# Splitting a norm and some maskings between engines, and a new order of loads, in a planned transformer kernel

## Chip, cores and metric

The kernel runs on one core of a Trainium2 chip. The metric is the device time of one execution in microseconds (us); of several executions the median is taken. The engines are called by their short names as well: PE is TensorE, DVE is VectorE, ACT is ScalarE, POOL is GpSimd and SP is SyncE, which here only issues DMAs.

## What is computed

Two sequences of 1024 tokens with 128 features pass six blocks, all in float32. Cut to what matters:

```python
x = x + 0.5 * L0_ffn(layernorm(x))            # mixes each token with the one before
x = x + L0_attn(layernorm(x))                 # 8 heads, full softmax
x = x + 0.5 * L0_ffn(layernorm(x))
x = x + 0.5 * L1_ffn(x)                       # "moe a": 16 experts, the best 2 for each token
x = x + L1_attn(x)                            # "scan": linear attention with decay
x = x + 0.5 * L1_ffn(x)                       # "moe b": the same experts once more
```

The scan keeps a state of 16 x 16 for each head, `state = state * beta + alpha * (k outer v)`, and its output is `q @ state`. An expert is `gelu(layernorm(h @ W1 + b1) * g1 + be1) @ W2 + b2`, weighted with the normalised router probability.

## The kernel before

The tokens lie in four groups G of 512 (four tiles of 128 tokens), two for each of the two sequences ("batches" b). All stages are generators that yield where they have to wait. A planner (`Plan`, from L74) keeps a modelled time of each engine and of each tile, and `step` takes the stage whose next piece can begin first. Engines run their instructions in the order in which the planner wrote them, so its constants decide the order on each engine: `SOON` (L82) is how far ahead it looks for a more urgent stage once attention is over, `late` and `delay` (L179 to L189) push a stage back, `note` (L134 to L169) is the modelled cost of an instruction, 0.45 us for a DMA issued by SP. LATE and GATHER at the end of the kernel give each stage of moe a, scan and moe b its delay; `behind` delays a quad by its turn.

Where TensorE would wait in the model, `Warm._fill` (L246 to L260) issues matmuls on zeros ("fillers", line L260 in the profile).

The stages that the change and the prediction touch:

- `norm` takes statistics on DVE, adds eps, and GpSimd raises to the power -0.5 (`rs`). Each of four tiles is then scaled by the engine named in `by`. A tile on ScalarE needs a bias, `sh = -mean * rs`, which GpSimd makes in two instructions. The norm of the scan's input has `by = ["DVE", "ACT"] * 2`; that of moe b, in `logits("b", ...)` at the end of `scan_out`, has `["DVE"] * TG`, all four on DVE.
- `route` finds for each token its two experts and its two rows in a table of slots in DRAM (`pos`), all on DVE with a few matmuls (`pc`). `scatter` (line L926 in the profile) writes the normed tokens to these rows (`x_slots`), 8 indirect DMAs for a group, issued by GpSimd one after the other. The pool queue is in order: a scatter, a power or a masking stands behind all that was written to GpSimd before it.
- `choose` finds which expert each of the extra 15 tiles belongs to (`eid`), and `quad` handles four tiles of 128 slots. For the first four quads the expert matrices lie in SBUF; the others fetch theirs with one DMA a tile (`wt<-w`), for which SP reads `eid`. Then SP loads the slots (`xg<-x_slots`), TensorE transposes (`pxT`), multiplies (`ph`), DVE and GpSimd make the norm (`hst`, `hmv`, `hrs`), DVE or ScalarE scales (`hn`, the split is chosen by the model), TensorE transposes (`phT`), ScalarE applies gelu (`act`), TensorE multiplies (`py`), and SP stores `y_slots<-y`.
- `gather` brings each token's two outputs back (`yt<-y_slots`), 16 indirect DMAs for a batch, issued by GpSimd; `combine` adds them to x on DVE, and in moe b SP stores the result.
- `scan_in` norms and transposes; `scan_pair` makes q and k of two chunks of 128 tokens, rotates them (`tm` on DVE, `qk` on GpSimd), scales and transposes them, and makes the scores in four banks `pj`. Each bank, 128 x 512, is masked with the causal matrix on DVE (`aj`), 16 maskings a batch. `scan_state` makes the states `S` from `pkv`, `scan_out` the outputs `po`, `oT_scan`, `pw`, and `x_scan` on DVE.

The order in the last 290 us is: moe a for batch 0 and 1, the scan of batch 0 while moe a of batch 1 ends, the scan of batch 1, moe b of batch 0 and 1, and the last gathers.

Each fetched matrix and the slot loads of a quad are issued so:

```python
for i, e in enumerate(experts_of(sp, eid, q)):
    ins = sp.dma_start(out=wt[:, i, :], in_=w12[bass.ds(e, 1), :, :].rearrange("a c d -> c (a d)"))
    ...
yield wait(("sent", s, 2 * b), ("sent", s, 2 * b + 1), banks=0, on="SP", issued=not own)
```

Of the kernel before, what the change touches and what calls it, by code (L numbers as in the profile page):

```python
# [14 lines left out]
ALU = mybir.AluOpType  # L15
# [7 lines left out]
TG = 4  # L23
# [9 lines left out]
def bc(ap, axis, n):  # L33

    u = ap.unsqueeze(axis)
    shape = list(u.shape)
    shape[axis] = n
    return u.to_broadcast(shape)
# [35 lines left out]
class Plan:  # L74
# [4 lines left out]

    by_engine, SOON = False, 0.3  # L82

    slow = 1.1
    RATE = 250.0
# [48 lines left out]
    def note(self, engine, op, args, kwargs):  # L134

        aps = [*args, *kwargs.values()]
        aps = [v.ap if isinstance(v, bass.IndirectOffsetOnAxis) else v for v in aps]
        aps = [v for v in aps if hasattr(v, "tensor")]
        out = kwargs.get("out", aps[0])

        ins = [v for v in aps if v is not out and v.space != DRAM]
        begin = self.free.get(engine, 0.0)
        for v in ins:
            hop = 0.0 if self.by.get(self._name(v)) == engine else self.HOP
            begin = max(begin, self.wrote.get(self._name(v), 0.0) + hop)
        if out.space == PSUM:
            begin = max(begin, self.wrote.get(self._name(out), 0.0))
        if "dma" in op:
            issued = max(begin, self.begun) + (1.25 if engine == "POOL" else 0.45)
            size = min(math.prod(out.shape), math.prod(kwargs["in_"].shape))  # L150
            moved = 4e-3 * size / self.RATE
            self.free["DMA"] = max(issued + 0.4, self.free.get("DMA", 0.0)) + moved
            end = self.free["DMA"] + 2.0
        else:
            issued = end = begin + (
                1.04 if ALU.pow in args else self.length(engine, op, out, ins)
            )
        self.free[engine] = issued
        for v in ins:
            k = self._name(v)  # L160
            self.used[k] = max(self.used.get(k, 0.0), end)
        k = self._name(out)
        self.wrote[k], self.by[k] = end, None if "dma" in op else engine
        self.used[k] = max(self.used.get(k, 0.0), end)
        self.end = max(self.end, end)
        self.issued = max(self.issued, issued)
# [49 lines left out]
def wait(*flags, **more):  # L216
    return {"for": flags, **more}
# [20 lines left out]
class Warm(Timed):  # L238
# [4 lines left out]
    zeros, ident, on = None, None, False  # L243
# [30 lines left out]
def kernel(ctx: ExitStack, tc: tile.TileContext, a, out):  # L274
# [5 lines left out]
    plan = Plan()  # L280
    in_order = InOrder(tc, nc.gpsimd)
    pe = Warm(plan, "PE", nc.tensor)
    dve, act, pool, sp = (
        Timed(plan, name, engine)
        for name, engine in (
            ("DVE", nc.vector), ("ACT", nc.scalar), ("POOL", in_order),
            ("SP", nc.sync),
        )
    )
# [32 lines left out]
    def tiles_of(t):  # L322
        return t.rearrange("p (n d) -> p n d", d=D)
# [139 lines left out]
    causal = const.tile([P, P], F32, name="causal", tag="causal")  # L463
# [81 lines left out]
    def norm(G, x, xn, by, twice=False):  # L545

        st = stat.tile([P, TG, nc.vector.BN_STATS_DIM], F32, tag=f"st{G}", name="st4")
        mv = stat.tile([P, TG, 2], F32, tag=f"mv{G}", name="mv4")
        for n in range(TG):
            latest["stats"] = dve.bn_stats(st[:, n, :], x[:, n, :]).ins  # L550
            dve.bn_aggr(mv[:, n, :], st[:, n, :])
        rs = stat.tile([P, TG], F32, tag=f"rs{G}", name="rs4")
        e = pool if "DVE" not in by else dve
        if twice:


            e.tensor_scalar(rs, mv[:, :, 1], 1.0 + EPS, EPS * EPS, ALU.mult, ALU.add)
        else:
            e.tensor_scalar(rs, mv[:, :, 1], EPS, None, ALU.add)
        if ("tile pools",) in plan.flags:  # L560
            yield wait(banks=0, on="POOL")
        pool.tensor_tensor(rs, rs, half_neg, ALU.pow)
        if "ACT" in by:
            sh = stat.tile([P, TG], F32, tag=f"sh{G}", name="sh4")
            pool.tensor_tensor(sh, mv[:, :, 0], rs, ALU.mult)
            pool.tensor_scalar(sh, sh, -1.0, None, ALU.mult)
        yield wait(banks=0, on=by[0])
        for n in range(TG):
            scale = rs[:, n : n + 1]
            if by[n] == "ACT":  # L570
                act.activation(
                    xn[:, n, :], x[:, n, :], AF.Identity, bias=sh[:, n : n + 1], scale=scale
                )
            else:
                engines[by[n]].tensor_scalar(
                    xn[:, n, :], x[:, n, :], mv[:, n, 0:1], scale, ALU.subtract, ALU.mult
                )
        yield wait(on="PE")
# [163 lines left out]
    xb_of, xm_of, xs_of, xn_of, xT_b, z_of, route_of = {}, {}, {}, {}, {}, {}, {}  # L742
# [273 lines left out]
    WINDOW, AHEAD = 6, 8  # L1016
# [9 lines left out]
    def quad(s, b, q, turn):  # L1026
# [3 lines left out]
        if own:  # L1030
            yield wait(
                ("w12",), ("tile pools",),
                *([("quad", turn - AHEAD)] if turn >= AHEAD else []), banks=0, on="SP",
            )
            mats = [(res["w1"][:, 4 * q + i, :], res["w2"][:, 4 * q + i, :]) for i in range(n)]
        else:
            yield wait(
                ("eid", s, b), ("tile pools",),
                *([("quad", turn - AHEAD)] if turn >= AHEAD else []), banks=0, on="SP",
            )  # L1040
            eid = eid_of[s, b]
            wt = tp.tile([P, TG, 2 * D], F32, tag=f"w{q % 4}", name="wt")
            for i, e in enumerate(experts_of(sp, eid, q)):
                ins = sp.dma_start(
                    out=wt[:, i, :], in_=w12[bass.ds(e, 1), :, :].rearrange("a c d -> c (a d)")
                )
                after(ins.ins, moved)
                if i < n - 1:
                    yield wait(on="SP", banks=0, issued=True, late=1.0)
            mats = [(wt[:, i, 0:D], wt[:, i, D:]) for i in range(n)]  # L1050
# [241 lines left out]
    def scan_pair(b, pair):  # L1292
# [49 lines left out]
        pj = [bank("pj") for j in range(4)]  # L1342
# [11 lines left out]
        for j in range(4):  # L1354
            where, tag = AM[pair % 2][j]
            aj = where.tile([P, 2, 2, P], F32, tag=tag, name="aj")
            dve.tensor_tensor(
                aj.rearrange("p i m t -> p (i m) t"), tiles_of(pj[j]), bc(causal, 1, 4), ALU.mult
            )
            done(pj[j])  # L1360
            am.append(aj)
        st["am", pair] = am
# [34 lines left out]
    def scan_out(G):  # L1397
# [37 lines left out]
        done(pw)  # L1435
        plan.set("scanned", G)
        yield wait(banks=0, on="DVE")
        yield from logits("b", G, xs_of[G], ["DVE"] * TG, "ACT")

# [243 lines left out]

    def behind(turn, late):

        return lambda: late + 0.8 * max(0, turn - sum(f[0] == "quad" for f in plan.flags))


    LATE = {"a": (2.0, 0.0), "scan": (-1, 0.5), "b": (3, 0.5)}
    GATHER = {"a": (0, 1), "b": (1.0, 1)}
    for s in ("a", "b"):
        for b in range(NB):
            late_by = LATE[s][b]
# [119 lines left out]
```

## Time and profile before

| | |
|---|---|
| median of 3 runs | 632.66 us (631.8 to 632.89) |
| the profiled execution | 633.37 us, of which its span is 631.3 |
| PE busy | 567.6 us (90%), 4418 matmuls |
| DVE busy | 461.9 us (73%), 1448 instructions |
| ACT busy | 291.3 us (46%), 626 |
| POOL busy | 284.9 us (45%), 345 |
| maskings `aj<-pj,causal` | 32 on DVE, 679 to 686 ns, between 446.1 and 516.2 us |
| norm of moe b `xn_moe_b` | 16 on DVE, 336 to 503 ns |
| biases `sh` of the scan's norm | on POOL, 198 to 202 ns and 228 to 238 ns (median) |
| fetched matrices `wt<-w` | 60 of 128 KB, 2.2 us to landing |
| slot loads `xg<-x_slots` | 32 (28 of 256 KB), 4.3 us to landing |
| indirect DMAs of POOL | 64 scatters and 64 gathers, near 1 us of issue each |

The span runs from the first to the last instruction. A group's busy time is the sum of its instructions; neighbours on one engine overlap in part, so the step from one to the next can be shorter than one lasts. The granted clock is that of TensorE, as a share of full speed.

### The profile page before, as it was taken

Reading aid. Unit: us, or ns where it says so; the run is one execution under the profiler, and the core shown is the slowest. Engines: PE = TensorE matmul, PEld = TensorE weight load, DVE = VectorE, ACT = ScalarE, POOL = GpSimd, SP = SyncE. Lnnn points to the kernel's source line nnn. Section 1 sums busy time; section 2 is a strip of 40 time slices with the busy share of each in tenths; the row PEclk is TensorE's granted clock in tenths of the full one; section 3 lists DMA queues with packets and bytes.
Section 4 is the critical chain, followed back from the end, with each engine's and each line's share of the span. In section 5 each row is a group of like instructions: output and inputs, shape, how many; then the busy total and the mean of one; then the engine's idle time right before and its main releaser. Section 6 shows DMA issues by size and latency. Waiting matters only on the chain.

```text
span 631.3 us, 12216 instructions
## 1 busy us (share of the span) xinstructions
PE 567.6 (90%) x4418; PEld 344.8 (55%) x4418; DVE 461.9 (73%) x1448; ACT 291.3 (46%) x626; POOL 284.9 (45%) x345
## 2 busy tenths in 40 slices
PE   8899999999999999989998998888897999999930
PEld 6664433333333434333346886777666867978820
DVE  6748887777867787788317883887897896777742
ACT  2442456655655465544781663575121201377720
POOL 5653000002613356204633847855744532675875
PEclk9887999999999999999998999999999896799985
DMA  4087000000202001000006437621200107237742
GB/s 121 4 295 202 1 2 2 1 1 1 69 2 67 1 1 35 1 2 9 26 2 179 123 102 205 177 73 42 65 9 1 35 23 219 86 101 227 225 120 72
DMA packets 62894, 46.22 MB, mean 73 GB/s; under 512 B 6241, under 2 KB 57841, under 8 KB 62833
## 3 DMA queue, kind: packets, MB, share of 16 engines
q1 hardware_dynamic: 58210, 36.78, 20.0%
q0 software_dynamic: 4096, 8.40, 4.7%
q8 instruction: 35, 0.57, 0.4%
q10 hardware_dynamic: 528, 0.26, 0.2%
q14 instruction: 25, 0.20, 0.1%
HBM read 26.94 MB, written 19.53 MB: 74 GB/s over the span
## 4 chain that ended last, share of the span: by engine, by line
PE 60%; DVE 21%; POOL 9%; issue 6%; DMA 3%; ACT 2%; POOLq 0%; ACTq 0%; DVEq 0%
PE sT L265 17%; PE av L265 10%; PE sc L265 7%; POOL x_slots L926 2%; POOL yt L65 2%; DVE tmp L233 2%; PE ph L265 2%; DVE hst L233 2%; PE py L265 2%; PE pk L265 2%; PE pt L260 2%; DMA yt<-y_slots,pos_moe_b 2%; PE pr L265 2%; PE pt L270 2%; DVE aj L233 2%
## 5 line engine op out<-in xcount | busy, mean ns | idle before, releaser
L233 DVE TENSOR_REDUCE tmp<-sc 128x1 f32<-128x512 f32 x256 | 162.3, 684 | 48.3 <-PE sc L265 47.9
L233 ACT ACTIVATE pT<-sT 128x512 f32<-128x512 f32 x256 | 137.7, 596 | 106.8 <-PE sc L265 85.6
L265 PE MATMUL sc<-kT,qT 32*128 32x512 f32 x512 | 151.8, 642 | 1.6 <-DVE rv L233 1.1
L265 PE MATMUL sT<-q,kT 32*128 32x512 f32 x512 | 135.4, 639 | 0.7 <-issue 0.7
L265 PE MATMUL av<-pT,va 128*32 128x256 f32 x1024 | 80.8, 390 | 0.0
L265 PEld LDWEIGHTS av<-pT,va 128*32 128x32 f32 x1024 | 21.2, 108 | 90.4 <-issue 89.1
L265 PEld LDWEIGHTS sT<-q,kT 32*128 32x128 f32 x512 | 37.7, 183 | 43.4 <-issue 29.8
L65 POOL TENSOR_TENSOR x_attn<-att,x_ffn_a 128x512 f32<-128x512 f32 x4 | 5.1, 1272 | 119.3 <-DVE att L233 119.3
L265 PEld LDWEIGHTS sc<-kT,qT 32*128 32x128 f32 x512 | 47.3, 185 | 15.4 <-ACT pT L233 6.1
L233 ACT ACTIVATE act<-phT,be,g 128x128 f32<-128x128 f32 x124 | 46.0, 465 | 8.7 <-PE phT L270 7.6
L926 POOL DMA_INDIRECT x_slots<-xn_moe_b,pos_moe_b x32 | 31.7, 991 | 29.2 <-issue 26.7
L926 POOL DMA_INDIRECT x_slots<-xn_moe_a,pos_moe_a x32 | 32.7, 1020 | 22.6 <-issue 14.2
L65 POOL TENSOR_TENSOR hrs<-hrs,half_neg 128x4 f32<-128x4 f32 (+1 forms) x32 | 32.7, 1022 | 11.0 <-DVE hrs L233 10.2
L65 POOL TENSOR_TENSOR rs<-rs,half_neg 128x4 f32<-128x4 f32 x24 | 25.3, 1054 | 23.7 <-DVE rs L233 22.6
L65 POOL DMA_INDIRECT yt<-y_slots,pos_moe_a x32 | 31.7, 991 | 9.4 <-issue 5.3
L65 POOL DMA_INDIRECT yt<-y_slots,pos_moe_b x32 | 31.1, 971 | 10.0 <-issue 6.2
L233 DVE BATCH_NORM_STATS2 hst<-ph 128x6 f32<-128x128 f32 x124 | 27.5, 283 | 5.2 <-PE ph L265 5.2
L270 PE MATMUL phT<-ident,hn 128*128 128x128 f32 x124 | 25.4, 296 | 5.6 <-DVE hn L233 4.2
L233 ACT COPY xgT<-pxT 128x512 f32<-128x512 f32 (+1 forms) x29 | 16.5, 581 | 27.9 <-PE pxT L270 27.9
L233 ACT ACTIVATE hn<-ph,hrs 128x128 f32<-128x128 f32 x55 | 17.1, 368 | 22.7 <-DVE hn L233 15.0
L233 DVE TENSOR_SCALAR hn<-ph,hrs 128x128 f32<-128x128 f32 x69 | 20.2, 343 | 7.7 <-POOL hrs L65 7.5
L233 DVE SCALAR_TENSOR_TENSOR x_moe_b<-yt,gate_moe_b,x_moe_b 128x128 f32<-128x128 f32 x32 | 11.1, 353 | 16.9 <-DMA yt<-y_slots,pos_moe_b 16.6
(362 smaller groups left out, 1082.9 us busy)
## 6 DMA issues: line engine op xcount, KB each, us to landing
wt<-w SPq DMA_DIRECT2D x60, 128.0 KB, 2.2
xg<-x_slots SPq DMA_DIRECT2D x28, 256.0 KB, 4.3
y_slots<-y SPq DMA_DIRECT2D x28, 256.0 KB, 2.6
x_slots<-zeros SPq DMA_DIRECT2D x2, 1792.0 KB
w_last<-in_w SPq DMA_DIRECT2D x1, 1024.0 KB, 16.9
w<-in_w SPq DMA_DIRECT2D x1, 1024.0 KB
w<-w SPq DMA_DIRECT2D x1, 1024.0 KB
out<-x_moe_b SPq DMA_DIRECT2D x4, 256.0 KB
```

Source lines behind the costliest of these rows:

```text
L65: r = method(*args, **kwargs)
L233: return method(*args, **kwargs)
L260: self._engine.matmul(*args, **kw)
L265: return self._engine.matmul(out, lhsT, rhs, **kwargs)
L270: return self._engine.transpose(out, in_, ident)
L926: ins = in_order.unordered.indirect_dma_start(**kw)
```

## The change

Four things are edited. A masking may go to ScalarE (a copy from PSUM to SBUF) and GpSimd (the multiplication, in place), where the model has these two finish it no later than DVE. The norm of moe b is done half by ScalarE, and once attention is over the bias is one DVE instruction in place of two on GpSimd. A fetched matrix is modelled as a longer issue and its stage gets `late=6.0`, so that slot loads can come in front of it on SP. And the planner's constants are set anew.

```diff
-    by_engine, SOON = False, 0.3
+    by_engine, SOON = False, 0.5
...
-            issued = max(begin, self.begun) + (1.25 if engine == "POOL" else 0.45)
+            moving = out.tensor.name.startswith("wt")
+            issued = max(begin, self.begun) + (
+                1.25 if engine == "POOL" else 0.65 if moving else 0.5
+            )
...
         if "ACT" in by:
             sh = stat.tile([P, TG], F32, tag=f"sh{G}", name="sh4")
-            pool.tensor_tensor(sh, mv[:, :, 0], rs, ALU.mult)
-            pool.tensor_scalar(sh, sh, -1.0, None, ALU.mult)
+            if ("tile pools",) in plan.flags:
+                yield wait(banks=0, on="DVE")
+                dve.scalar_tensor_tensor(sh, mv[:, :, 0], -1.0, rs, ALU.mult, ALU.mult)
+            else:
+                pool.tensor_tensor(sh, mv[:, :, 0], rs, ALU.mult)
+                pool.tensor_scalar(sh, sh, -1.0, None, ALU.mult)
...
-                *([("quad", turn - AHEAD)] if turn >= AHEAD else []), banks=0, on="SP",
+                *([("quad", turn - AHEAD)] if turn >= AHEAD else []), banks=0, on="SP", late=6.0,
...
-            dve.tensor_tensor(
-                aj.rearrange("p i m t -> p (i m) t"), tiles_of(pj[j]), bc(causal, 1, 4), ALU.mult
-            )
+            flat = aj.rearrange("p i m t -> p (i m) t")
+
+            if plan.free["DVE"] + 0.68 < max(plan.free["ACT"] + 0.84, plan.free["POOL"]) + 1.22:
+                dve.tensor_tensor(flat, tiles_of(pj[j]), bc(causal, 1, 4), ALU.mult)
+            else:
+                act.copy(flat, tiles_of(pj[j]))
+                pool.tensor_tensor(flat, flat, bc(causal, 1, 4), ALU.mult)
...
-        yield from logits("b", G, xs_of[G], ["DVE"] * TG, "ACT")
+        yield from logits("b", G, xs_of[G], ["DVE", "ACT"] * 2, "ACT")
...
-        return lambda: late + 0.8 * max(0, turn - sum(f[0] == "quad" for f in plan.flags))
+        return lambda: late + 0.6 * max(0, turn - sum(f[0] == "quad" for f in plan.flags))
...
-    LATE = {"a": (2.0, 0.0), "scan": (-1, 0.5), "b": (3, 0.5)}
-    GATHER = {"a": (0, 1), "b": (1.0, 1)}
+    LATE = {"a": (2.0, 0.0), "scan": (-1.0, 0.5), "b": (2.0, 0.5)}
+    GATHER = {"a": (0.0, -2.0), "b": (1.0, 1.0)}
```

Counted over all instructions as the two kernels are built: of 32 maskings 10 go to ScalarE and GpSimd (4 of batch 0, 6 of batch 1); 8 of the 16 tiles of moe b's norm go to ScalarE; 8 biases are made by DVE, and GpSimd makes 4 fewer pairs. By the planner's choice 13 of 55 `hn` go from ScalarE to DVE, and 85 fillers are issued instead of 89. The order of the instructions differs throughout the last 290 us.

## The prediction

> **What bounds the kernel now.** I read the page, then busy time in stretches of 5 us, then the chain of waits and the timelines of those stretches. On the page no single engine is the bound.
>
> ```profile
> span 631.3 us, 12216 instructions
> ...
> PE 60%; DVE 21%; POOL 9%; issue 6%; DMA 3%; ACT 2%; POOLq 0%; ACTq 0%; DVEq 0%
> ...
> L65 POOL TENSOR_TENSOR x_attn<-att,x_ffn_a 128x512 f32<-128x512 f32 x4 | 5.1, 1272 | 119.3 <-DVE att L233 119.3
> ```
>
> Up to about 340 us (attention) the two kernels issue the same instructions in the same order but for a few swaps, so the change acts on the last 290 us. The stretches show what limits there. Columns: length; PE, weight load, DVE, ACT and POOL busy with counts; granted clock; DMA share; GB/s.
>
> ```profile
> 440.00:445.00 5.00, 5.00 (x65) 4.61 (x63) 1.78 (x7) 3.53 (x11) 3.78 (x5) 1.00 0.28 78
> 445.00:450.00 5.00, 4.81 (x86) 3.86 (x78) 4.86 (x13) 0.00 (x0) 3.78 (x5) 1.00 0.25 65
> 460.00:465.00 5.00, 4.74 (x66) 2.65 (x57) 4.93 (x13) 0.67 (x2) 0.51 (x1) 1.00 0.07 16
> 505.00:510.00 5.00, 3.91 (x53) 2.20 (x43) 4.77 (x14) 0.00 (x0) 0.00 (x0) 1.00 0.00 0
> 525.00:530.00 5.00, 5.00 (x20) 4.08 (x19) 3.53 (x19) 0.93 (x4) 1.15 (x2) 0.50 0.70 197
> 540.00:545.00 5.00, 5.00 (x27) 5.00 (x25) 2.59 (x17) 1.76 (x3) 3.78 (x5) 0.52 0.17 56
> 545.00:550.00 5.00, 5.00 (x42) 4.87 (x41) 3.39 (x17) 2.10 (x6) 3.22 (x4) 1.00 0.13 41
> ```
>
> VectorE is full in both scans (445 to 465, 495 to 520) while ScalarE is empty and GpSimd has holes. From 525 to 545 TensorE is full at half clock. The chain shows the hole on GpSimd in the second scan, and the end:
>
> ```profile
> 503.94 9.19 issue
> 513.12 0.96 POOL x_slots L926
> ...
> 625.11 2.49 DMA yt<-y_slots,pos_moe_b
> 627.68 0.35 DVE x_moe_b L233
> ```
>
> The end is GpSimd's: 16 gathers of the last batch, 1.26 us apart, start when the last batch's expert outputs are stored (604.98). Whatever brings that point forward moves the end by as much.
>
> **The masked scores.** Of 32 maskings 10 leave VectorE: 4 of 16 in the first scan, 6 in the second. One takes 681 ns, four in a row 2.48 us, so each is worth (2.48 - 0.68)/3 = 0.60. For the first scan that is 2.4 us, for the second 3.6. What they cost elsewhere: a ScalarE copy of 128x512 from PSUM (0.58, the row of oT_scan), on an engine that idles there, and 1.27 on GpSimd.
>
> Also in the first scan VectorE now gets three maskings before it turns to the state; before, it sat idle there:
>
> ```profile
> 443.20 0.61 DVE L233 SCALAR_TENSOR_TENSOR S<-pkv,decay,blk 128x128 f32<-128x128 f32 x2 [3.15 <-PE pkv L265]
> ```
>
> TensorE computes those scores ahead of pkv in the new order, so 3 x 0.60 = 1.8 us fall into a hole of 3.15.
>
> Against this stands a rule and its row. A GpSimd operation and a VectorE operation with two SBUF inputs exclude each other:
>
> ```profile
> 478.53 0.72 POOL L65 TENSOR_TENSOR qk<-tm 128x256 f32<-128x256 f32 x1 [0.80 <-DVE tm L233]
> ```
>
> ```profile
> 478.61 0.72 DVE L233 TENSOR_TENSOR eqa_moe_b<-z_moe_b,top_moe_b 128x64 f32<-128x64 f32 x1
> 479.37 0.22 DVE L233 TENSOR_TENSOR eqa_moe_b<-eqa_moe_b,rev 128x64 f32<-128x64 f32 x1
> ```
>
> The first comparison takes 0.72 instead of 0.22 and ends just after GpSimd's 0.72. The Trainium skill (SBUF — State Buffer, "SBUF: two separate sides") says that the shared ports are a lock held for a whole instruction. By the rule each GpSimd masking can hold VectorE for its 1.27: 12.7 us in all, twice the gain. By the row it holds only an operation with two SBUF inputs that arrives meanwhile, for what is left. A masking on VectorE itself reads PSUM and one SBUF tile and isn't of that kind; the state's sums (S<-S), the gathered outputs (x_moe_a) and the routing are. I take 0.35 a masking, near the row's 0.5 but not met every time: 1.4 us in the first scan, 2.1 in the second (range 0 to 12.7).
>
> Behind a masking GpSimd's queue holds gathers and scatters. In the second scan three stand ahead of the second group's first scatter, in the 9.19 us hole, and cost nothing if the hole is 3.8 us; two stand among its scatters, 2 x (1.27 + 0.2) = 2.9 us. But the positions these scatters need come after 5 maskings fewer on VectorE (-3.0). Net about 0.
>
> **The norms.** Of the last norm 8 of 16 tiles go to ScalarE: 8 x 0.26 (four in a row took 1.11) = 2.1 us off VectorE; two on ScalarE take 0.88 beside two on VectorE. All 8 biases, these four and those of the scan's norm, are one VectorE instruction on 128x4; none such is in the trace. The nearest row, a tensor_scalar on 128x4, takes 0.17 (0.42 when held), so 8 x 0.17 = 1.4 us added (1 to 3.4). GpSimd loses 4 x (0.20 + 0.24 + gaps), some 2 us, at places where ScalarE waited for it 5.4 us in three waits, mostly off the path. For the path of the norm itself: bias 0.17 and a hop, then 0.88 on ScalarE, against 1.11 before: 0.
>
> **The order.** The planner's constants move more than the named edits. In the instruction orders:
> - Hidden units scaled by ScalarE fall from 55 to 42; 13 x 0.26 = 3.4 us return to VectorE, in the expert stages. It is 70 to 90% busy there and I charge nothing; without that cover up to 3.4.
> - On SP single slot loads move in front of fetched matrices in the first layer's first batch (after 4 matrices, not 9). TensorE is 95 to 100% busy from 345 to 375, so I charge 0.
> - In its second batch one hrs power (1.24 with its gap) moves ahead of the scatters whose last (386.16, landed 388.7) released the slot loads: -1.2. But SP now issues its first six matrices behind the seventh store of outputs (384.95 before, when the matrices had gone at 377.25) and four more behind the eighth, 4 x 0.6 = 2.4, and the slot loads after those. The two cancel if the seventh store comes some 3 us earlier, as TensorE's order lets it. I take 0 (from -1.2 to +2.4).
> - In the second scan's input the add of bo1 (1.27 on GpSimd) moves behind two rotations. VectorE waited 2.42 us for the first of them. Against it ScalarE's half of the norm comes after more VectorE work; I take -0.5.
> - In the last layer the expert numbers of its first batch are ready ahead of the second group's last norm, so its 13 (before 12) matrices start earlier than 520.85. Those 12 took 8.33 us, and only then, at 529.5, came the slot loads. SP can be there some 3.5 us earlier, but the scatters then end last, and TensorE is at half clock and full. Between 519 and 551 the 16 fillers (about 1 us each at half clock, 0.46 at full) become 5, while two gate products of 3.1 us each move in, one from later. I take -1.0 (from -4 to +3).
>
> **Sum.** First layer 0, first scan -2.4 - 1.8 + 1.4 = -2.8, its hand-over -0.5, second scan -3.6 + 2.1 = -1.5, last layer -1.0, last gathers 0: -5.8. The profiled execution took 633.37 for a span of 631.3; so 625.5 + 2.07 = 627.6. The median of the three runs, 632.66, lies 0.7 below that execution: 626.9.
>
> **Rivals.**
> 1. *GpSimd's lock takes the gain.* If each of the ten maskings meets an operation with two SBUF inputs at its start, it costs about 1.0 (1.27 less the 0.22 they would take): 10.0 against my 3.5. The sum is +0.7: 633.4. For it: the row above. Against: most of what VectorE does then reads PSUM. 0.12.
> 2. *The clock.* The fill matmuls keep the clock up, and 11 of 16 go. TensorE stayed at half clock from about 524.4 to 544.9 although busy. The skill (TensorE: Matmul & The Clock Gate, "What's actually happening") has full clock back after a busy window of about 3.4 us; by that a shut gate costs 1.7 us of work, by the row 10. If the gaps that lose their filler keep the gate shut until 565, half of TensorE's 20 us is added, 10 us, and the result is 636.9. It decides from 5.8/0.5 = 12 us more at half clock. For it: the row contradicts the quick release. Against: slots arrive earlier and leave less idle time. 0.17.
> 3. *The scans gain and nothing else loses.* With no lock (-3.5) and the slot loads worth their 3.5 (-2.5 more), the sum is -11.8: 620.9. For it: ScalarE and GpSimd are empty beside the maskings. Against: the lock's row, and the scatters that end last. 0.17.
> 4. *The edits do what they say, off the path.* The first scan's gain ends in the rope and rotation chain (470 to 495, VectorE 80% busy), and the last layer waits for the same scatters: only the second scan and the last layer count, -2.5: 630.2. 0.16.
>
> **Numbers.** My forecast has 0.38: with rivals 3 and 4 faster is 0.71, plus a little of rival 1. What a measurement of this kernel can tell from no change is about 0.2%, 1.3 us: 631.4 to 633.9. Same: most of rival 1, 0.10. Slower: rival 2 and a lock dearer than I priced, 0.18. The range runs from 619 to 635: from rival 3, with the scatter's 1.2 as well, to rival 2 in a mild form.
>
> **What would show it.** DVE idle before the first S gone, or cut by half; x_scan of the last group near 516 instead of 520.5 (-4.8); ten GpSimd maskings of 1.27, with S<-S and x_moe_a beside them at 0.35 (mine) or near 1 (rival 1); the half-clock stretch no longer than 20 us (mine) or past 560 (rival 2); the last gathers as close as before, 1.26 us, beginning near 599. I am wrong if the scans end no earlier, or if the last gathers begin at 605 though they do.

## The result and the profile after

The changed kernel takes 636.63 us (median of 11 executions, 634.76 to 641.10), the kernel before 632.66 (11 executions of the same session, 629.49 to 635.05). The ratio is 1.0074, with a 95% interval from 1.0050 to 1.0098: slower by 4.0 us, where 626.9 was forecast. The profiled execution of the changed kernel is the shortest of its eleven, 634.76 with a span of 633.0, and that of before lies 0.7 above its median. So the two traces differ by only 1.7 us of span, and the other 2.3 us of the result can't be looked up in them.

The page of the changed kernel, head and busy times:

```profile
span 633.0 us, 12222 instructions
...
PE 561.6 (89%) x4410; PEld 341.7 (54%) x4410; DVE 461.9 (73%) x1450; ACT 297.5 (47%) x632; POOL 295.7 (47%) x347
```

VectorE is as busy as before (461.9). Summed by instruction, its maskings and norm tiles fell by 9.7 us and `hn` and biases rose by 6.0; but `S<-S` and `x_moe_a`, as many as before, took 5.2 us more, because GpSimd held some of them, as is shown below. GpSimd has 10.8 us more. Where the time is lost shows in stretches of 5 us (columns: length; PE, weight load, DVE, ACT, POOL busy with counts; granted clock; DMA share; GB/s):

```profile
410.00:415.00 5.00, 3.12 (x20) 2.35 (x18) 4.89 (x23) 3.14 (x9) 4.30 (x4) 1.00 0.21 66
415.00:420.00 5.00, 4.85 (x20) 4.57 (x20) 1.68 (x7) 2.99 (x9) 0.00 (x0) 0.52 0.17 52
...
510.00:515.00 5.00, 1.57 (x14) 1.07 (x14) 3.65 (x17) 0.00 (x0) 1.59 (x3) 0.58 0.00 0
515.00:520.00 5.00, 5.00 (x93) 4.19 (x92) 1.95 (x4) 1.76 (x3) 1.94 (x2) 0.74 0.10 30
...
540.00:545.00 5.00, 5.00 (x23) 4.49 (x23) 3.77 (x20) 1.17 (x2) 1.03 (x1) 0.51 0.44 116
```

In 510 to 515, where TensorE was busy 4.94 us before, it is busy 1.57, and the clock falls in that stretch and the next. A second such place lies at 410 to 420, ahead of the first scan, where TensorE waits 1.75 us for `hn`. The kernel before has a hole there too, of 1.49 us, and keeps its clock:

```profile
410.00:415.00 5.00, 3.51 (x26) 2.77 (x24) 4.97 (x16) 2.36 (x7) 4.62 (x5) 1.00 0.47 131
415.00:420.00 5.00, 4.87 (x33) 4.24 (x33) 4.12 (x18) 4.99 (x15) 0.99 (x2) 1.00 0.00 0
```

The timeline of the changed kernel's second scan shows the reason for the wait there. VectorE:

```profile
502.17 2.12 DVE L237 SCALAR_TENSOR_TENSOR S<-S,decay 128x128 f32<-128x128 f32 x1
...
507.02 1.00 DVE L237 SCALAR_TENSOR_TENSOR S<-S,decay 128x128 f32<-128x128 f32 x1
...
508.32 0.97 DVE L237 SCALAR_TENSOR_TENSOR S<-S,decay 128x128 f32<-128x128 f32 x1
509.22 0.21 DVE L237 TENSOR_TENSOR over_moe_b<-pc,steps 128x64 f32<-128x64 f32 x1
...
509.72 0.75 DVE L237 TENSOR_TENSOR_SCAN upto_moe_b<-one,upto_moe_b,nt_moe_b 128x16 f32<-128x16 f32 x1
...
512.69 0.68 DVE L237 TENSOR_TENSOR aj<-pj,causal 128x512 f32<-128x512 f32 x1
```

Before, all four maskings of this pair of tiles stand ahead of the routing, which begins with `over_moe_b`:

```profile
506.62 2.48 DVE L233 TENSOR_TENSOR aj<-pj,causal 128x512 f32<-128x512 f32 x4
509.01 0.21 DVE L233 TENSOR_TENSOR over_moe_b<-pc,steps 128x64 f32<-128x64 f32 x1
```

The changed kernel's GpSimd, and its TensorE, in the same stretch:

```profile
506.60 3.83 POOL L65 TENSOR_TENSOR aj<-aj,causal 128x512 f32<-128x512 f32 x3
```

```profile
513.43 1.07 PE L269 MATMUL po<-aj,vp 128*32 128x128 f32 x12 [3.82 <-DVE aj L237]
...
516.16 2.75 PE L269 MATMUL pj<-qTs,kTs 32*128 32x128 f32 x64
```

A sum `S<-S` takes 0.35 when free and the running total `upto_moe_b` 0.25, so these four VectorE instructions were held 1.77, 0.65, 0.62 and 0.50 us, 3.5 in all, beside GpSimd's maskings. That uses up what the maskings sent away had freed: the routing begins at 509.22, no earlier than before. Of the four maskings of this pair of tiles three went to GpSimd in a row; the fourth stayed on VectorE, where it stands behind the held sums and the whole routing of the group, until 512.69; the routing alone puts 3.5 us in front of it. TensorE waits 3.82 us for it, then works at half clock, and VectorE waits 4.13 us in turn for the next scores (518.05).

The chain still ends as before: gathers 1.26 us apart, then

```profile
626.43 2.51 DMA yt<-y_slots,pos_moe_b
...
629.04 0.35 DVE x_moe_b L237
```

The last `x_scan` begins at 526.2 (before 520.5, forecast near 516), the first gather of the last batch at 606.0 (before 605.0, forecast near 599).

A table by stage compares all kernels. The stages are cut at the last `x_attn`, the last `x_scan` of the first scan, the scales of the second scan, its last `x_scan`, and the first gather of the last batch's outputs. Chip R is that of the result; the later runs came to five others, and on four of them the kernel before takes not 633 but 666 to 672. The last column is the start of that gather. Each row is one profiled execution, and executions differ: on chip 3, `e_row` and `e_fill` have the same instructions up to the last `x_attn` and reach it at 350.3 and 345.2.

| kernel | chip | to x_attn | moe a, first scan | hand-over | second scan | moe b | sum |
|---|---|---|---|---|---|---|---|
| before | R | 337.6 | 130.9 | 25.4 | 26.6 | 84.5 | 605.0 |
| changed | R | 338.4 | 131.1 | 24.2 | 32.5 | 79.8 | 606.0 |
| e_noslots | 5 | 336.7 | 134.2 | 24.4 | 33.2 | 81.6 | 610.1 |
| e_norm | 5 | 338.9 | 131.0 | 29.9 | 27.4 | 83.2 | 610.4 |
| before_d | 4 | 340.5 | 144.5 | 26.2 | 41.3 | 86.8 | 639.3 |
| changed (after_b) | 2 | 345.6 | 144.0 | 24.5 | 37.3 | 86.0 | 637.4 |
| changed (after_c) | 3 | 349.2 | 144.9 | 24.3 | 35.6 | 85.3 | 639.3 |
| e_consts | 1 | 346.5 | 148.2 | 25.8 | 43.1 | 87.3 | 650.9 |
| e_edits | 1 | 341.9 | 138.1 | 23.2 | 32.2 | 97.2 | 632.5 |
| e_frozen_dve | 1 | 349.7 | 146.8 | 27.5 | 43.5 | 81.5 | 649.0 |
| e_frozen_dve2 | 1 | 349.6 | 144.3 | 24.2 | 43.4 | 81.3 | 642.8 |
| e_consts_b | 2 | 342.6 | 144.6 | 24.2 | 43.8 | 86.2 | 641.3 |
| e_edits_b | 2 | 342.1 | 140.4 | 23.2 | 34.1 | 93.3 | 633.2 |
| e_frozen_dve2_b | 2 | 348.0 | 142.8 | 25.1 | 39.4 | 85.1 | 640.4 |
| e_row | 3 | 350.3 | 142.4 | 24.4 | 35.7 | 81.3 | 634.1 |
| e_fill | 3 | 345.2 | 140.3 | 24.3 | 34.6 | 84.9 | 629.3 |
| e_best | 4 | 345.2 | 140.6 | 24.2 | 34.2 | 81.0 | 625.2 |
| e_edits_c | 3 | 340.8 | 138.9 | 23.2 | 34.3 | 98.1 | 635.3 |
| e_order | 4 | 343.3 | 149.5 | 21.5 | 44.1 | 80.5 | 638.9 |
| e_slots | 4 | 350.8 | 143.6 | 27.9 | 41.5 | 91.6 | 655.4 |

On chip R the second scan loses 5.9 us, moe b takes 4.7 of it back, and the rest is small. On chips 1 to 4 the second scan has the other sign: it takes 32.2 to 37.3 us in the eight profiles that send some of its maskings away, and 39.4 to 44.1 in the eight that send none.

### The profile page after: what moved, and what is told of

It is laid out like the page before. It is cut to its first block, busy times and chain, and to the rows that moved or that the text cites. A ratio compares the mean times of both kernels' runs of the same rounds, so it can differ in the third digit from the quotient of the medians.

```text
span 633.0 us, 12222 instructions
## 1 busy us (share of the span) xinstructions
PE 561.6 (89%) x4410; PEld 341.7 (54%) x4410; DVE 461.9 (73%) x1450; ACT 297.5 (47%) x632; POOL 295.7 (47%) x347
## 4 chain that ended last, share of the span: by engine, by line
PE 55%; DVE 24%; POOL 8%; issue 6%; DMA 4%; ACT 1%; SPq 1%; POOLq 0%; ACTq 0%; DVEq 0%
PE sT L269 17%; PE av L269 10%; PE sc L269 6%; POOL yt L65 2%; DVE tmp L237 2%; POOL hrs L65 2%; PE py L269 2%; PE pt L264 2%; DVE hst L237 2%; DVE S L237 2%; PE pk L269 2%; POOL x_slots L934 1%; DVE st L237 1%; PE pr L269 1%; DVE x_moe_a L237 1%
## 5 line engine op out<-in xcount | busy, mean ns | idle before, releaser
L237 ACT ACTIVATE pT<-sT 128x512 f32<-128x512 f32 x256 | 137.7, 596 | 106.8 <-PE sc L269 86.3
L269 PEld LDWEIGHTS sT<-q,kT 32*128 32x128 f32 x512 | 37.7, 183 | 43.4 <-issue 28.9
L65 POOL DMA_INDIRECT yt<-y_slots,pos_moe_b x32 | 30.9, 965 | 13.8 <-issue 8.8
L65 POOL TENSOR_TENSOR hrs<-hrs,half_neg 128x4 f32<-128x4 f32 (+1 forms) x32 | 32.5, 1017 | 9.2 <-DVE over_moe_a L237 5.0
L65 POOL TENSOR_TENSOR rs<-rs,half_neg 128x4 f32<-128x4 f32 x24 | 25.8, 1075 | 16.1 <-DVE rs L237 10.9
L237 DVE TENSOR_SCALAR hn<-ph,hrs 128x128 f32<-128x128 f32 x82 | 23.8, 344 | 9.2 <-POOL hrs L65 9.1
L237 DVE BATCH_NORM_STATS2 hst<-ph 128x6 f32<-128x128 f32 x124 | 27.4, 282 | 3.3 <-PE ph L269 3.3
L274 PE MATMUL phT<-ident,hn 128*128 128x128 f32 x124 | 24.3, 293 | 4.3 <-DVE hn L237 3.2
L237 ACT ACTIVATE hn<-ph,hrs 128x128 f32<-128x128 f32 x42 | 13.2, 369 | 20.0 <-DVE hn L237 18.1
```

The lines of the kernel that those rows point to most:

```text
L65: r = method(*args, **kwargs)
L237: return method(*args, **kwargs)
L269: return self._engine.matmul(out, lhsT, rhs, **kwargs)
L274: return self._engine.transpose(out, in_, ident)
```

## The experiments

Three theories. A: the maskings on GpSimd lose the time, by holding VectorE and by standing in a row that TensorE waits for. B: the new order (the planner's constants) loses what the edits gain. C: the clock that falls after TensorE's two holes costs it. Ratios are to the kernel before on the same chip, with 95% intervals.

### Chip 1 (before 672.28): order and edits apart

**e_consts**: before with the new constants only.

```diff
-    by_engine, SOON = False, 0.3
+    by_engine, SOON = False, 0.5
...
-            issued = max(begin, self.begun) + (1.25 if engine == "POOL" else 0.45)
+            moving = out.tensor.name.startswith("wt")
+            issued = max(begin, self.begun) + (
+                1.25 if engine == "POOL" else 0.65 if moving else 0.5
+            )
...
-                *([("quad", turn - AHEAD)] if turn >= AHEAD else []), banks=0, on="SP",
+                *([("quad", turn - AHEAD)] if turn >= AHEAD else []), banks=0, on="SP", late=6.0,
...
-        return lambda: late + 0.8 * max(0, turn - sum(f[0] == "quad" for f in plan.flags))
+        return lambda: late + 0.6 * max(0, turn - sum(f[0] == "quad" for f in plan.flags))
...
-    LATE = {"a": (2.0, 0.0), "scan": (-1, 0.5), "b": (3, 0.5)}
-    GATHER = {"a": (0, 1), "b": (1.0, 1)}
+    LATE = {"a": (2.0, 0.0), "scan": (-1.0, 0.5), "b": (2.0, 0.5)}
+    GATHER = {"a": (0.0, -2.0), "b": (1.0, 1.0)}
```

> This is the kernel before with only the planner's new constants (how soon a step may begin, the price of a DMA's issue, the lateness of fetched matrices, of quads, layers and gathers); all 32 maskings, the last norm and the bias stay as before. Theory A (the maskings on GpSimd lose the time: GpSimd holds VectorE's S sums and TensorE waits for masked scores in the second scan): without them the new order is level with before or a little faster, 630 to 633.5. Rival B (the new order loses the time, above all by the idle stretch of TensorE ahead of the first scan, 410 to 415 us, after which the clock falls; the maskings are neutral): as slow as the change or slower, 636 to 639.

**e_edits**: before with its constants, and the edits of maskings, norm and bias as in the change. Its planner sends 9 maskings away.

> This is the kernel before with its own constants and only the named edits: maskings by ScalarE and GpSimd where the planner's rule chooses so (9 of 32), half of the last norm on ScalarE, the bias on VectorE. Theory A: slower than before, 635 to 638, with S sums of 1 to 2 us beside GpSimd's maskings in the second scan and the last x_scan some 5 us later than before's 520.5. Rival B: faster than before, 628 to 632, since the scans gain what VectorE no longer does.

**e_frozen_dve**: the changed kernel, its order of instructions frozen, but each masking that was sent away is done by VectorE. It stands there where the planner had written the copy and the product, so some of these maskings stand behind the routing.

```diff
-                act.copy(flat, tiles_of(pj[j]))
-                pool.tensor_tensor(flat, flat, bc(causal, 1, 4), ALU.mult)
+                plan.note("ACT", "copy", (flat, tiles_of(pj[j])), {})
+                plan.note("POOL", "tensor_tensor", (flat, flat, bc(causal, 1, 4), ALU.mult), {})
+                nc.vector.tensor_tensor(flat, tiles_of(pj[j]), bc(causal, 1, 4), ALU.mult)
```

> The changed kernel with the order of all instructions kept as planned, but each of the ten maskings done by one VectorE instruction at the place where ScalarE's copy and GpSimd's product stood. Theory A: the second scan ends 3 to 5 us earlier (last x_scan near 522 instead of 526.2), the first 2 to 3 later; the last layer, which in the changed kernel made up most of the delay, leaves 0 to 2 us: 634.5 to 636.6. Rival B: the second scan ends no earlier, and the time is that of the change or up to 3 us more.

**e_frozen_dve2**: the same under `if b == 1`, so for the second scan alone.

> As before this one, but only the second scan's six maskings go back to VectorE; the first scan's four stay on ScalarE and GpSimd. Theory A: the best of the two, the first scan as in the change (469.5) and the second some 4 us earlier: 632 to 635. Rival B: no difference from the change, 636 to 637.

Measured: e_consts 1.0126 (1.0096 to 1.0156), e_edits 0.9869 (0.9833 to 0.9905), e_frozen_dve 1.0099 (1.0062 to 1.0136), e_frozen_dve2 0.9976 (0.9952 to 1.0000). So here theory B holds: the constants alone lose 1.3%, the edits alone gain 1.3%, and the first scan's four maskings are worth 1.2% (the two frozen kernels differ in these alone). But the kernel before itself took 672 here, not 633.

### Chip 2 (before 665.82): the same beside the changed kernel

**after_b** is the changed kernel; the other three are the kernels above again.

> The changed kernel once more, to stand beside the parts on one chip. In the first four runs the kernel before took 672 and not 633 (a chip on which loads of expert matrices and slots landed some 10 us later), the named edits alone 0.987 of it, the new constants alone 1.013. Theory A (maskings on GpSimd lose the time) expects a ratio over that of the second scan's maskings undone (0.998): 1.00 to 1.01. Theory B (the new order loses what the edits gain): the product of both parts, 0.987 x 1.013 = 1.000, or the 1.007 measured at first.

> The named edits alone with the constants of before, a second time. Theory B: 0.985 to 0.99 of before again, on any chip. Theory A: on a chip where before takes 633, slower than before, 1.003 to 1.008; the gain of 1.3% is then one of that chip alone.

> The new constants alone, a second time. Theory B: 1.01 of before or more again. Theory A: within 0.3% of before on a chip where before takes 633.

> The changed kernel's order with the second scan's six maskings back on VectorE, a second time, now beside the changed kernel on the same chip. Theory A: 0.3 to 0.7% less than the changed kernel. Theory B: within 0.2% of it or slower.

Measured: after_b 0.9934 (0.9888 to 0.9980), e_edits_b 0.9944 (0.9905 to 0.9983), e_consts_b 1.0084 (1.0043 to 1.0125), e_frozen_dve2_b 1.0002 (0.9955 to 1.0049). The changed kernel is faster here. Undoing the second scan's six maskings loses 4.2 us by the medians (665.06 against 660.86), against theory A; the intervals of the two ratios overlap (0.9955 to 0.9980).

Yet the hold of theory A is in the trace of after_b, even clearer. Three maskings in a row on GpSimd, and a running total of 128x16 on VectorE, which takes 0.25 when free:

```profile
528.67 3.70 POOL L65 TENSOR_TENSOR aj<-aj,causal 128x512 f32<-128x512 f32 x3
```

```profile
528.46 3.97 DVE L237 TENSOR_TENSOR_SCAN upto_moe_b<-one,upto_moe_b,nt_moe_b 128x16 f32<-128x16 f32 x1
```

Here it wasn't held for what was left of one GpSimd instruction (1.27), but for the whole row of three. That is one of five profiles with this row. In the other four (`after`, `after_c`, `e_fill`, `e_noslots`) VectorE gets in between the three. In `after_c` the instructions with two SBUF inputs are held for one masking each (1.21 and 1.05, usually 0.23), and one that reads PSUM isn't held:

```profile
533.65 1.21 DVE L237 TENSOR_TENSOR slot_moe_b<-slot_moe_b,skip_moe_b 128x64 f32<-128x64 f32 x1
534.78 0.21 DVE L237 SCALAR_TENSOR_TENSOR behind_moe_b<-pc,skip_moe_b 128x64 f32<-128x64 f32 x1
535.03 1.05 DVE L237 TENSOR_TENSOR slot_moe_b<-slot_moe_b,behind_moe_b 128x64 f32<-128x64 f32 x1
```

So the hold takes VectorE's time, and on this chip something larger stands against it.

### Chip 3 (before 670.75): the row and the clock

**e_row**: the frozen form above under `if b == 1 and pair == 1`, so that only the three maskings in a row go back to VectorE. **e_fill**: ten fill products that the planner doesn't know of, so its order stays; three ahead of the transposes `phT` of one quad, seven in `scan_out`, which add zeros to `po`.

```diff
+        if turn == 11:
+            for _ in range(3):
+                nc.tensor.matmul(pt[:, 0:256], pe.ident, pe.zeros, start=True, stop=True)
...
+            if G == 2 and n == 2:
+                for _ in range(7):
+                    nc.tensor.matmul(
+                        po[:, 256:512], pe.ident, pe.zeros, start=False, stop=False,
+                        skip_group_check=True,
+                    )
```

> The changed kernel a third time, to be compared on one chip with the three beside it. On the chip of the result it took 1.007 of before (633), on another, where before takes 666, 0.993. If the sign goes with the chip, 1.007 where before takes 633, and 0.99 to 1.00 where it takes 665 to 672.

> The changed kernel in its own order, only the three maskings that stand in a row on GpSimd in the second scan (its second pair of tiles) go back to VectorE; the other seven stay. Theory A, now in a sharper form: a VectorE operation with two SBUF inputs that meets a row of GpSimd operations is held until the whole row has ended (3.5 us of S sums and running totals held in the changed kernel's first profile, 3.75 in the second, where one running total took 3.97 for 0.22). Undoing the row removes 3.5 and adds 3 x 0.6: the last x_scan 2 to 4 us earlier, the time 0 to 3 us less than the changed kernel's, since the last layer made up for most of such delays. Theory B (the order loses, the maskings gain): the time 0 to 2 us more.

> The changed kernel in its own order with ten fill products on TensorE in its two holes: three of zeros ahead of the hidden units' transposes after the first scan's first input (idle from 412 to 414 us), seven that add zeros to po of the second scan's first half, where it waits for the masked scores (509.6 to 513.4). Theory C (the clock that falls after these two holes costs the time): the granted clock stays at 1.0 from 415 to 421 and from 510 to 517, the first S comes 2 to 3 us earlier, the time is 2 to 4 us less than the changed kernel's. If the clock only follows the waits: within 0.2% of it or up to 2 us more.

> The named edits alone with the constants of before, a third time: 0.987 and 0.994 of before on two chips where it takes 672 and 666. Theory B: below 1 again, 0.985 to 0.995. Theory A on a chip where before takes 633: 1.002 to 1.008.

Measured: after_c 0.9924 (0.9897 to 0.9951), e_row 0.9891 (0.9856 to 0.9927), e_fill 0.9883 (0.9823 to 0.9944), e_edits_c 0.9914 (0.9883 to 0.9944). Each repair comes out 0.3 to 0.4% below the changed kernel, in the sense of A and of C, but the intervals overlap.

e_row doesn't gain where theory A said. The hold is gone, and from the scales to the positions of the second group it takes 17.9 us in place of 20.4. But its second scan is no shorter (35.7 against 35.6 in after_c), since the three maskings stand behind the routing on VectorE as well, and TensorE waits for them:

```profile
534.81 2.85 PE L269 MATMUL po<-aj,vp 128*32 128x128 f32 x16 [3.35 <-DVE aj L1373]
```

Its gain lies in moe b, 81.3 us against 85.3, where TensorE has the higher clock. That stage as one stretch, in after_c and then in e_row:

```profile
553.99:639.30 85.31, 77.87 (x498) 68.04 (x497) 62.90 (x302) 44.21 (x115) 49.66 (x52) 0.86 0.54 154
```

```profile
552.81:634.10 81.29, 70.70 (x497) 62.14 (x496) 62.79 (x301) 43.80 (x114) 49.04 (x51) 0.95 0.56 162
```

Why it has that clock there wasn't found out. What e_fill does to the clock is plain. The stretches around the first hole, in after_c and then in e_fill, where the stage comes some 4 us earlier:

```profile
430.00:435.00 5.00, 3.12 (x23) 2.69 (x22) 4.90 (x24) 3.33 (x9) 4.60 (x5) 1.00 0.27 79
435.00:440.00 5.00, 4.72 (x22) 4.07 (x23) 2.75 (x11) 3.79 (x11) 0.75 (x1) 0.71 0.17 52
```

```profile
425.00:430.00 5.00, 4.36 (x28) 3.16 (x26) 4.93 (x21) 3.13 (x10) 3.59 (x4) 1.00 0.15 45
430.00:435.00 5.00, 5.00 (x39) 4.79 (x39) 3.31 (x10) 2.51 (x9) 1.05 (x2) 1.00 0.17 52
```

Three fill products keep the clock at 1.0 where it fell to 0.71, and moe a with the first scan takes 140.3 us in place of 144.9. Not all of these 4.6 us are the fill's, for e_row, which has no fill, takes 142.4. But the effect repeats: the hole of 1.75 us is in all seven profiles of this order without the fill, and in each the clock falls to 0.5 within 2.5 us of its end, for 3.4 to 6.9 us; in the two with it (e_fill and e_best) the clock stays. From the last `x_attn` to the scales of the first scan those two take 106.7 and 106.8 us, and the six without it on chips 1 to 3 109.2 to 111.3.

### Chip 4 (before 672.17): which constants, and both repairs

**before_d** is the kernel before; **e_slots** is before with `late=6.0` and the dearer DMA issue alone, **e_order** before with the other constants alone; **e_best** is e_row and e_fill together.

> The kernel before, unchanged, for its trace on a chip of the kind on which it takes 665 to 672: its milestones beside those of the changed kernel there (first S at 465 to 470, last x_scan at 551 to 554, last gathers of outputs from 637 to 639) show in which stage the change gains there. If the maskings gain what the new order loses, before's first S comes earlier than 463 and its second scan ends later than 5 us behind that lead; if the gain lies in the last layer, its last gathers begin at 645 or later while the scans are level.

> The kernel before with one half of the new constants: fetched matrices issued later than slot loads (late by 6 us), and the dearer price of a DMA's issue. All engines' work as before. The new constants together cost 1.3 and 0.8% on two chips. If the queue of loads is what costs, this half alone takes 1.005 to 1.015 of before; if the lateness of layers and gathers costs, 0.997 to 1.003.

> The other half: how soon a step may begin, the lateness of quads, layers and gathers; loads queued by the rule of before. If the queue of loads costs, 0.997 to 1.003 of before; if this half costs, 1.005 to 1.015.

> The changed kernel with both repairs: the row of three maskings back on VectorE, and the ten fill products in the two holes. On the third chip the first alone gave 0.989, the second 0.988, the changed kernel 0.992 of before. If the lock and the clock are separate losses, 0.984 to 0.988; if they are one (the clock falls because of the wait that the row makes), 0.988 to 0.991. On a chip where before takes 633: 1.000 to 1.004.

Measured: before_d one execution, 668.35; e_slots 1.0128 (1.0081 to 1.0176), e_order 0.9988 (0.9963 to 1.0012), e_best 0.9829 (0.9786 to 0.9871). Here the rule for loads makes the whole loss of the constants. Both repairs together are 1.7% better than before and about 1% better than the changed kernel was on the chips before (0.9924, 0.9934); the intervals no longer meet. That is a little more than was expected of two separate losses, so the two gains seem to add up, though the single repairs were measured on another chip. In the stages e_best has both: 140.6 us in moe a and the first scan, as e_fill, and 81.0 in moe b, as e_row.

In before_d the first S comes at 451.7 (465 to 470 in the changed kernel), and the last `x_scan` at 552.5 is level with it (551.4 and 554.0). Of the lead 5 to 9 us lie before the last `x_attn`, where the programs hardly differ. Counted from there, the changed kernel is 8 to 9 us behind at the first S and 6 to 7 ahead at the last `x_scan`. So the first of the two cases holds: there the scans with fewer maskings on VectorE win back more than the new order loses before them.

The trace also shows one thing that differs on these chips. Waits of TensorE for nothing that the profile shows ("issue"; us in total, times, longest), in before_d and then in before on chip R, where this is the only such row:

```profile
PE po L265 <- issue: 3.9, 7, 1.0
PE pj L265 <- issue: 2.3, 4, 0.9
...
PE pkv L265 <- issue: 1.6, 2, 1.0
```

```profile
PE sT L265 <- issue: 0.7, 1, 0.7
```

All rows of before_d sum to 12.9 us in 22 waits; the changed kernel has 0.7 on chip R, 4.9 on chip 2 and 9.6 on chip 3, and e_noslots and e_norm have 0.7 on chip 5. In before_d most of them fall on the scans' many small products (`po`, `pj`, `pkv`), and the clock falls after them as after a hole (two waits of 0.3 and 0.9 us at 519.5 to 521.2, then 0.50 from 525 to 530). Before's second scan takes 41.3 us here against 26.6 on chip R. In the eight profiles on chips 1 to 4 that send none of its maskings away TensorE is at half clock for 17 to 27 us of it, in the eight that do for 3 to 13; on chip R it was 0 before and 6.8 in the changed kernel. That these waits make the difference is argued, not shown: what TensorE waits for is not in the trace, and e_row has more of them (13.1 us) than after_c and is no slower.

### Chip 5 (before 633.25): two last kernels

**e_noslots**: the changed kernel without `late=6.0` and the dearer issue, planned anew (10 maskings away again). **e_norm**: before with only the norm's edits:

```diff
-            pool.tensor_tensor(sh, mv[:, :, 0], rs, ALU.mult)
-            pool.tensor_scalar(sh, sh, -1.0, None, ALU.mult)
+            if ("tile pools",) in plan.flags:
+                yield wait(banks=0, on="DVE")
+                dve.scalar_tensor_tensor(sh, mv[:, :, 0], -1.0, rs, ALU.mult, ALU.mult)
...
-        yield from logits("b", G, xs_of[G], ["DVE"] * TG, "ACT")
+        yield from logits("b", G, xs_of[G], ["DVE", "ACT"] * 2, "ACT")
```

> The changed kernel planned anew without its rule for loads (fetched matrices late by 6 us, a DMA's issue dearer), with all the rest of the change: ten maskings, norm, bias, the other constants. By itself that rule costs 1.3%, the other constants nothing (0.999), the named edits gain 0.6 to 1.3%. If these add up, 0.985 to 0.992 of before, that is as good as the changed kernel (0.992) or up to 0.7% better; if the rule costs only in the order of before, 0.992 to 1.000.

> The kernel before with only the norm's part of the change: half of the last norm on ScalarE, all biases of this kind made by VectorE; all 32 maskings on VectorE, constants of before. The named edits together take 0.987 to 0.994. If the maskings make that gain, 0.997 to 1.003; if the bias taken from GpSimd makes it, 0.988 to 0.996.

Measured: e_noslots 1.0076 (1.0046 to 1.0106), e_norm 1.0075 (1.0050 to 1.0101). Both expectations missed, and this chip is of the kind of chip R. The rule for loads, which cost 1.3% by itself on chip 4, is not what makes the change slow here: without it the ratio is that of the change. And the norm's edit, which I had thought neutral, costs 0.75% alone.

In e_noslots the second scan repeats what chip R showed: the row, the held sum, TensorE's wait (33.2 us against 26.6).

```profile
503.78 2.12 DVE L234 SCALAR_TENSOR_TENSOR S<-S,decay 128x128 f32<-128x128 f32 x1
```

```profile
508.93 3.77 POOL L65 TENSOR_TENSOR aj<-aj,causal 128x512 f32<-128x512 f32 x3 [0.75 <-ACT aj L234]
```

```profile
515.49 1.07 PE L266 MATMUL po<-aj,vp 128*32 128x128 f32 x12 [2.80 <-DVE aj L234]
```

In e_norm, with all maskings on VectorE, that scan takes 27.4. Its loss is in the hand-over (29.9 against 25.4). VectorE makes the bias, and then the tiles of the norm come 2.5 us later:

```profile
468.02 0.16 DVE L233 SCALAR_TENSOR_TENSOR sh<-mv,rs 128x4 f32<-128x4 f32 x1 [0.69 <-POOL rs L65]
...
470.50 0.59 DVE L233 TENSOR_SCALAR xn_moe_b<-x_scan,mv,rs 128x128 f32<-128x128 f32 x2
```

```profile
470.89 1.12 PE L270 MATMUL pt<-ident,xn_moe_b 128*128 128x128 f32 x4 [2.73 <-DVE xn_moe_b L233]
```

The edit adds a `yield` between the power and the tiles. Between bias and tiles the planner lets another group's statistics (eight instructions, 1.7 us), an `rs` and an `x_scan` (0.68) onto VectorE. TensorE waits 2.73, and then is slow for 14 us although it has work:

```profile
470.00:475.00 5.00, 4.11 (x17) 3.57 (x18) 3.70 (x16) 0.59 (x1) 3.42 (x4) 0.54 0.00 0
475.00:480.00 5.00, 5.00 (x23) 4.46 (x22) 2.61 (x12) 2.13 (x5) 0.00 (x0) 0.50 0.00 0
480.00:485.00 5.00, 5.00 (x22) 4.29 (x21) 1.37 (x5) 1.23 (x3) 2.08 (x3) 0.60 0.00 0
```

## Why the prediction was wrong

By its own steps, on chip R (trace against trace, span +1.7):

- **"Up to about 340 us ... a few swaps"**, priced 0: +0.8 at the last `x_attn`. Small, and present within the first 60 us.
- **"First layer 0"**: +2.8 more at the first scan's scales (436.8 to 440.4). After the hole at 410 to 415 (TensorE busy 3.12 of 5) the clock is at half until about 422. `pba`, `pv` and `pq` of the first scan begin 2.1 us ahead of before's, but take 7.45 us where before took 4.09. I had priced orders and queues there, and no hole of TensorE.
- **First scan -2.8**: right. From its scales to its last `x_scan` 31.7 became 29.1, -2.6. The hole of 3.15 us in front of the state is now filled by three maskings. Holds there are small: `x_moe_a` sums of 1.84 beside a masking and of 1.20 beside a rotation (`qk`), where 0.73 is usual, so 1.1 us are the maskings', against the 1.4 forecast.
- **Hand-over -0.5**: -1.2, right in kind. The bias's price and the norm's "0" hold in this order, where the tiles follow the bias at once (468.40, then 468.6); e_norm shows that in another order the same edit costs 4.5.
- **Second scan -1.5**: the step that failed; +5.9. "three stand ahead of the second group's first scatter, in the 9.19 us hole, and cost nothing if the hole is 3.8 us" is true of GpSimd's own queue alone. Three things were left out or too small. A single masking and the row hold VectorE 3.5 us in all, where I had put 6 x 0.35 = 2.1. The maskings were counted as a sum of VectorE time saved, but `po` needs the last of the four, and that one stood on VectorE behind the routing; that the positions would come 3.0 us earlier turned into 0.7 later (512.6). And the wait it makes (3.82) costs again through the clock: the two `po` and the `pj` after it take 4.63 us, before 3.21.
- **Last layer -1.0**: -4.7; the term was mis-sized, and 0.7 beyond its bound of -4. Moe b made up for part of the late start: it took 84.5 us before, and 81.6 in e_noslots, which starts late too and has no rule for loads, so that rule is at most some 2 us of it. How little an early end of the scans is worth there shows on chip 3: with before's constants, e_edits_c ends them 16.8 us ahead of after_c and begins the last gathers 4.0 ahead.
- **Last gathers 0**: +0.7 from their start to the end of the span.

The sum is +0.8 + 2.8 - 2.6 - 1.2 + 5.9 - 4.7 + 0.7 = +1.7. The difference of the medians, 4.0, holds 2.3 more that no trace shows; all executions of the changed kernel have a mean clock of 0.928 to 0.939, and the profiled ones 0.939 against 0.945 before.

Of the rivals, *the clock* came nearest (636.9), but not by its mechanism as put: the half-clock stretch in moe b got shorter (530 to 545, before 525 to 545), and new ones came after new waits, at 415 and 510. Summing twice the missing clock over the stretches from 335 to 610 gives 30.9 us before and 37.7 after, not the 12 more from which I let it decide. *The lock* was right in the second scan in size (3.5 us for four maskings, near the 1.0 for each that it put), and in the first it was as small as I had taken it.

What stays open. That the second scan's maskings cause the loss on chips of this kind rests on traces: two kernels with the row lose 5.9 and 6.6 us there against before, one without it 0.8. Undoing the row was tried only on the other kind, where the six maskings together gain. No run moved the last masking ahead of the routing, and none filled the holes on a chip like R, so how the 5.9 us divide between the hold, the place of that masking and the clock is read from one trace. Why those chips take 33 to 40 us more, and why the change is faster there (0.9924 and 0.9934) though slower on chip R, is not settled: the waits of TensorE for nothing shown may be part of it. e_best was run there only; that it would beat before on a chip like R isn't shown.

## What to carry to other kernels

Work that goes to another engine is worth what its last piece is worth: find out who waits for the last of the set, on which engine that last piece stands, and what stands before it there. A GpSimd masking of 1.27 us held a VectorE operation with two SBUF inputs beside it by 0.5 to 1.8 us in the changed kernel, so count which operations of that kind stand there. A new wait in an order that a planner writes is a place where other work gets in; look at what stands behind it on the engine before you price it at nothing. And a short hole of TensorE, here 1.75 us, can cost more in clock than in idle time, so try to fill it.

## What the runs showed of the hardware

- In four of five profiles with three maskings in a row on GpSimd, VectorE's instructions with two SBUF inputs were held for one masking at a time (1.21 and 1.05 us for 0.23 in after_c). This agrees with the Trainium skill (SBUF — State Buffer, "SBUF: two separate sides"), which has the ports locked for a whole instruction. In after_b the hold lasted over the whole row: 3.97 us for an instruction of 0.25 beside three maskings of 3.70. In the changed kernel's first profile a held instruction even began at 502.17, before the recorded start of the masking at 502.84.
- A hole of TensorE of 1.75 us was followed by half clock in seven profiles of seven, one of 1.49 us at the same place (before, chip R) was not.
- A hole of TensorE of 2.73 us was followed by a clock of 0.54, 0.50 and 0.60 in three stretches of 5 us, in two of which TensorE was busy 5.00 of 5 (e_norm, 470 to 485). The Trainium skill (TensorE: Matmul & The Clock Gate, "What's actually happening") has full clock back after a busy window of about 3.4 us, from which I estimate 1.7 us of lost work for such a hole. The trace doesn't agree, if what the profile counts as busy is what that window counts.
- One program, two kinds of chip: the changed kernel's span is 633.0 on chip R, 664.6 and 666.6 on chips 2 and 3, with the same instructions. Sums of TensorE's waits for nothing shown: 0.7, 4.9 and 9.6 us. The sign of a change of 0.7% went with the chip.
